# Starting the norm of image 1 when the scans end, in a two-layer SSM and attention kernel

## The chip, the cores and the metric

The kernel runs on one core of a Trainium2 chip, in one launch. A core has TensorE (PE, matrix products), VectorE (DVE), ScalarE (ACT), GpSimd (POOL) and the sync engine (SP), each with an instruction queue of its own that runs in order, and 16 DMA engines that move data between HBM and the on-chip memory. A DMA stands in the queue of the engine that issues it: its waits are spent there. The metric is the device time of one execution in microseconds (us), as the median of several runs. The profile is one execution seen by the hardware profiler.

## The reference

The input x is 4 images of 96 channels and 128 x 128 points, in float32. Two layers are added to it, each behind a group norm `_gn` (32 groups of 3 channels).

Layer 0 is a state-space block:

```python
z = silu(dwconv3x3(in_w @ gn(x) + in_b) + dw_b)       # 192 channels
xs = [z, z transposed, and both reversed]             # 4 directions, L = 16384
dts, B, C = x_proj(xs)                                # rank 6, 1, 1
delta = softplus(dt_proj(dts) + bias);  dA = exp(delta * A)
h[t] = dA[t] * h[t-1] + delta[t] * B[t] * xs[t]       # the scan
y = h * C + D * xs                                    # summed over directions
x = x + out_w @ layernorm_over_channels(y) + out_b
```

Layer 1 is a convolutional attention block on the new x:

```python
xr, x1, x2 = relu_split_norm(gn(x))       # two passes: statistics, then two maps
key, qry = unfold(conv3x3(x1, aw1)), unfold(conv3x3(x2, aw2))
w = softmax(sum over patches(key * qry) / sqrt(96 * 9))    # a 96 x 96 x 3 x 3 filter per image
y1 = layernorm(conv3x3(conv3x3(x1, aw3), w))
y2 = layernorm(conv3x3(x2, w_conv2)) * x1
x = x + xr + w_full @ [y1, y2] + b_full
```

All of it is computed for each image. No image needs another's result; within an image each norm needs the whole image before it.

## The kernel before, in words

The work is written as Python generators, each of which emits instructions and yields an estimate of the TensorE time that they cost. `co_run(left, right, pace)` draws from a left generator, and for each unit of its cost lets the right one emit `pace` units. Two are thus woven into one stream.

**Projections** (`project`, L612): image after image, in 16 strips of 8 rows. A strip is loaded (`strip_in`), normalised in place on ScalarE (`stacked`, L455), copied with shifts by DMA (L463), and multiplied on TensorE in three groups `q` of seven terms `i`. The group norm of an image needs its statistics first: `image_stats` loads the image in 32 tiles (`xst`, L401) and takes `bn_stats` on VectorE (L404). Image 0's are taken ahead; those of images 1 to 3 run `beside` the projection of image 0, a half tile at each `next(beside, None)`.

**Scans** (`ssm_scan`): 384 steps of 1024 points on 128 channels. A step has products that spread B, C and delta (`to_psum`, L726), softplus and exp on ScalarE (L655, L788), a multiplication by u on GpSimd (`times_u`, L812), two halves of multiply, scan, multiply on VectorE (L816, L833, L837), and an addition into y on GpSimd (`into_y`, L845). The scans are the right generator `last` beside the projections, then beside the norm of image 0 (pace 0.5), then beside the nine taps of image 0 (pace 0.95).

**Norm** (`Image.norm`): `ssm_output`, then `split_norm`. `ssm_output` goes over 16 chunks of 1024 points. For chunk c it loads y (`load_y`, L929), squares it on ScalarE (`squares`, L934), sums y and its squares over the channels on TensorE (`sums`, L940), copies the sums out (`rows`, L950) and turns them into an 8 x 128 tile `mq` with two small DMAs (L953). One chunk later it takes the variance (`inverse`, L957 to L959), the root (`roots`, L963) and the reciprocal (`back`, L967), writes that to memory (`rd`, L969) and reads it back spread over 96 partitions (`spread_out`, `r`, L977). One chunk later still it projects (`projected`, L983), scales and adds (`scaled`, L991 to L993) and stores x (L1028). `split_norm` then makes two passes: relu and sums (L1077 to L1084), a small chain of single-column operations with one product (L1093), and the maps x1 and x2 (L1160, L1165), which are written to memory.

**Nine taps** (`direct_maps`, L1646): the three 3 x 3 convolutions of image 0 as nine shifted products each, strip by strip of three rows, with `Taps` turning the results (L1383) and multiplying patches (L1398). Its end is the softmax of the weights (`Taps.weights`, L1446 to L1462).

**Attention**: `attention(img)` does the same convolutions for images 1 to 3 in another form (L1288, L1299), with input sums made on GpSimd and VectorE (`columns`, L1264 to L1273), and for every image the convolution with the softmax weights. Beside the attention of image b run, as right generator `light`, the closing stage of image b-1 (`attn_output`) and the norm of image b+1.

What sets the order: from the first projection to the end of the scans and nine taps, `in_order` ties every instruction to the one emitted before it on its engine, so the written order is the order. Behind that point a scheduler chooses an order on each engine by its own estimates. The norm of image 0 draws its product banks from a pool of three (`psl`), the norms of images 1 to 3 from a pool of two (`psr`). All DMAs of these stages stand in the sync queue, apart from the weight tables (L246, L249), which GpSimd issues.

Of the kernel before, what the change touches and what calls it, by code (L numbers as in the profile page):

```python
# [14 lines left out]
PSUM = bass.MemoryType.PSUM  # L15
# [47 lines left out]
def kernel(  # L63
# [271 lines left out]
    def chain(*gens):  # L335
        for g in gens:
            yield from g

    def drain(gen):
        for _ in gen:  # L340
            pass
# [48 lines left out]
    def image_stats(b, pool):  # L390

        stats = pool.tile([C, NCH, 6], F32, name="stats", tag="stats")
        mv = const.tile([C, 2], F32, name=f"stats{b}", tag=f"stats{b}")

        def run(p2, ahead):
            xf = x[b].rearrange("c h w -> c (h w)")
            tiles = []
            for i in range(NCH + ahead - 1):
                if i < NCH:
                    tiles.append(p2.tile([C, CH], F32, name="xst", bufs=ahead))  # L400
                    nc.sync.dma_start(tiles[-1], xf[:, bass.ts(i, CH)])  # L401
                yield 0.7
                if i >= ahead - 1:
                    nc.vector.bn_stats(stats[:, i - ahead + 1], tiles.pop(0))  # L404
                yield 0.7
            nc.vector.bn_aggr(mv, stats.rearrange("p c s -> p (c s)"))

        return mv, run

    def project(b, weights, mv, beside, zb, xrows, ps):  # L410
# [8 lines left out]
        SP = ZR * PW + 2  # L419
        last = H // ZR - 1  # L420
        with tc.tile_pool(name="a2", bufs=2, side="left") as p2:
            beside = chain(*(run(p2, 2) for run in beside))
            later, parts = Later(), {}
            y0s = []
            for i in range(2):
# [173 lines left out]
            for s in range(last + 1):  # L599
                nxt = None  # L600
                z1 = p2.tile([128, NU, ZR, UW], F32, name="z1")
                z2 = p2.tile([128, NU, R, UW], F32, name="z2")
                for q in range(3):
                    pz = bank(ps)
                    for i, (k, d) in enumerate(terms):
                        n = C + KK + 1 if k == 2 else 128
                        if q < 2:
                            jobs = [(0, 128, 0, q)]
                        else:
                            jobs = [(0, 64, 128, 0), (64, 128, 128, 1)]  # L610
                        for p, e, c, at in jobs:
                            nc.tensor.matmul(  # L612
                                blocks(pz[p:e]),
                                lhsT=ws[k][:, d, c : c + e - p],
                                rhs=window(ys[k], at, d, n),
                                start=(i == 0),
                                stop=(i == len(terms) - 1),
                            )
                        if i in (2, 4, 6):
                            yield tick(2.6 if i == 2 else 1.8)  # L620
                        if i == 2 and q == 0 and s < last:
                            ahead = strip_in(s + 1)
                        if i in (2, 4, 6):
                            next(beside, None)
                    to = z1[:, :, q * R : (q + 1) * R] if q < 2 else z2
                    silu(to.rearrange("p b h w -> p b (h w)"), pz)
                    if q == 0 and s < last:
                        nxt = stacked(s + 1, *ahead)
                    if q == 1:
                        if before:  # L630
                            rp = rows_out(*before)
                            later(lambda a=before: z_out(*a), 1)
                            yield tick(1.8)
                        for _ in range(3):
                            next(beside, None)
                    if q == 2 and before:
                        cols_out(rp, before[2])
                        yield tick(1.3)
                before = z1, z2, s
                ys = nxt  # L640
                ready[b] = s - 1
# [272 lines left out]
    def ssm_output(b, yms, xnew, stats, ps, side):  # L914
# [5 lines left out]
        with tc.tile_pool(name="c2", bufs=2, side=side) as p2:  # L920
# [10 lines left out]
            def squares(c):  # L931
                sq = p2.tile([C, 2, SN], F32, name="sq", bufs=1)
                for j in range(2):
                    nc.scalar.activation(sq[:, j], ys[c][:, j], AF.Square)  # L934
                sums_of[c] = sq, bank(ps)
# [12 lines left out]
            def rows(c):  # L948
                st = p2.tile([128, CH], F32, name="st", bufs=1)
                nc.scalar.copy(st, sums_of.pop(c)[1])  # L950
                mq = made[c] = p2.tile([RS, 2, W], F32, name="mq")
                for i in range(2):
                    nc.sync.dma_start(mq[:, i], st[32 * i : 32 * i + 65 : 64])  # L953

            def inverse(c):
                m, q = made[c][:, 0], made[c][:, 1]
# [8 lines left out]
            def back(c):  # L965
                q = made.pop(c)[:, 1]
                nc.vector.reciprocal(q, q)  # L967
                to = rd[bass.ts(c, SN)]
                nc.sync.dma_start(to.rearrange("(p f) -> p f", f=W), q)  # L969
                xr = p2.tile([C, SN], F32, name="xr")  # L970
                nc.sync.dma_start(xr, xb[:, bass.ts(c, SN)])
                near[c] = xr, to

            def spread_out(c):
                xr, to = near[c]
                r = p2.tile([C, SN], F32, name="r")
                nc.sync.dma_start(r, to.partition_broadcast(C))  # L977
                near[c] = xr, r

            def projected(c, h):  # L980
# [17 lines left out]
            for c in range(NS + 2):  # L998
                new, old = c < NS, c - 2 if c >= 2 else None
                mid = c - 1 if 1 <= c <= NS else None  # L1000
                if old is not None:
                    po = projected(old, 0)
                yield 1.2
                if mid is not None:
                    inverse(mid)
                    roots(mid)
                if new:
                    squares(c)
                if old is not None:
                    scaled(old, 0, po)  # L1010
                    po = projected(old, 1)
                    ys.pop(old)
                if mid is not None:
                    back(mid)
                yield 1.4
                if new:
                    sums(c, 0)
                if mid is not None:
                    spread_out(mid)
                yield 1.4  # L1020
                if old is not None:
                    scaled(old, 1, po)
                    load_y(c + 1)
                if new:
                    sums(c, 1)
                yield 1.4
                if old is not None:
                    nc.sync.dma_start(xnew[:, bass.ts(old, SN)], near.pop(old)[0])  # L1028
                yield 1.4
                if new:  # L1030
                    rows(c)
                yield 1.4
# [766 lines left out]
    def projections(images, weights, stats, wp, ps):  # L1799
        for b in images:  # L1800
            beside = []
            for i in range(1, NB) if b == 0 else ():
                stats[i], run = image_stats(i, wp)
                beside.append(run)
            yield from project(
                b, weights, stats[b], beside, zb[b // 2][b % 2], xrows[b], ps
            )
            ready[b] = H // ZR
# [4 lines left out]
    with tc.tile_pool(name="wp", bufs=1, side="left") as wp:  # L1813
# [1 line left out]
        stats[0], run = image_stats(0, wp)  # L1815
        weights = project_weights(wp)
        with tc.tile_pool(name="a0", bufs=8, side="right") as p2:
            drain(run(p2, 8))
        first = len(traced())
        others = other_weights()  # L1820
        for images, pace in (([0], 0.25), ([1], 0.75), ([2, 3], 1.35)):
# [18 lines left out]
    co_run(left, last, 0.5)  # L1840
    drain(left)
    left = direct_maps(imgs[0], psl)
    co_run(left, last, 0.95)
    drain(left)
    drain(last)
    in_order(first)
    early.close()
    istats.append(ctx.enter_context(tc.tile_pool(name="istats1", bufs=1, side="left")))
    const = ctx.enter_context(tc.tile_pool(name="const2", bufs=1, side="left"))
    wful = load(w_full, "wful")  # L1850
    m96 = filled(1.0 / C, "m96", 128, 128)
# [4 lines left out]
        nc.vector.memset(mrows[i][0:64], rows / (H * C))  # L1856
        nc.vector.memset(mrows[i][64:128], (H - rows) / (H * C))
    psl = ctx.enter_context(tc.tile_pool(name="psa", bufs=6, space=PSUM, side="left"))
    psr = ctx.enter_context(tc.tile_pool(name="psr", bufs=2, space=PSUM, side="right"))
    wp = ctx.enter_context(tc.tile_pool(name="wpairs", bufs=1, side="left"))  # L1860
    pairs = [stacked_weights(wp, wd, f"wd{i}") for i, wd in enumerate(four)]
    for b in range(NB):
        light = []
        if b:
            light.append(imgs[b - 1].close(psr, "right"))
        if b + 1 < NB:
            imgs[b + 1] = Image(b + 1)
            light.append(imgs[b + 1].norm(yms[(b + 1) // 2][(b + 1) % 2], psr, "right"))
        light = chain(*light)
        left = imgs[b].attend(psl)  # L1870
        co_run(left, light, 0.5 if b else 1.5)
        drain(left)
        drain(light)
# [76 lines left out]
```

## Time and profile before

The median of 3 runs is 6911.25 us (6910.0 to 6920.79). The profiled execution spans 6917.3 us.

| stage, us from the start | length | TensorE busy | clock granted |
|---|---|---|---|
| projections, 0 to 2090 | 2090 | 1771 | 0.93 |
| norm of image 0 beside scans, 2090 to 2571 | 481 | 240 | 0.60 |
| nine taps beside scans, 2571 to 3361 | 790 | 750 | 0.98 |
| rest of the nine taps, 3361 to 3436 | 75 | 75 | 1.00 |
| softmax of image 0's weights, 3436 to 3487 | 51 | 27 | 0.64 |
| output of image 0 beside norm of image 1, 3487 to 3908 | 421 | 270 | 0.76 |
| attention of image 1, 3908 to 4946 | 1038 | 868 | 0.91 |
| attention of image 2, 4946 to 5989 | 1043 | 873 | 0.90 |
| attention of image 3 and closing, 5989 to 6917 | 928 | 788 | 0.93 |

Over the whole span TensorE is busy 82%, VectorE 71%, ScalarE 42%, GpSimd 49%. The stages have different limits, so the table is to be read row by row. A wait in the profile is named by the waiting instruction, then what ended the wait, then the total, the count and the longest in us. `issue` is time in which the engine waited for nothing that the profile shows.

### The profile page before, as it was taken

Reading aid. Unit: us, or ns where it says so; the run is one execution under the profiler, and the core shown is the slowest. Engines: PE = TensorE matmul, PEld = TensorE weight load, DVE = VectorE, ACT = ScalarE, POOL = GpSimd, SP = SyncE. Lnnn points to the kernel's source line nnn. Section 1 sums busy time; section 2 is a strip of 40 time slices with the busy share of each in tenths; the row PEclk is TensorE's granted clock in tenths of the full one; section 3 lists DMA queues with packets and bytes.
Section 4 is the critical chain, followed back from the end, with each engine's and each line's share of the span. In section 5 each row is a group of like instructions: output and inputs, shape, how many; then the busy total and the mean of one; then the engine's idle time right before and its main releaser. Section 6 shows DMA issues by size and latency. Waiting matters only on the chain. (4 is left out here: it accounts for less than half of the span.)

```text
span 6917.3 us, 74304 instructions
## 1 busy us (share of the span) xinstructions
PE 5662.7 (82%) x22236; PEld 2330.5 (34%) x22236; DVE 4920.7 (71%) x6916; ACT 2913.8 (42%) x3685; POOL 3397.6 (49%) x2072
## 2 busy tenths in 40 slices
PE   5879979878886629999977488987788987888987
PEld 2323323322221114444422234443334442334432
DVE  3357779989896678788466675568765568775688
ACT  1247778777875476676312321232121232121102
POOL 1126758879794239778222233434433334444641
PEclk9989989989996659999978799997899997899998
DMA  7666677866766666766567765667665666565556
GB/s 171 169 155 172 177 208 199 232 170 171 218 181 169 182 200 193 200 180 175 163 183 192 201 167 149 181 169 202 172 166 146 178 170 201 157 173 137 139 155 175
DMA packets 798510, 1227.60 MB, mean 177 GB/s; under 512 B 217726, under 2 KB 557702, under 8 KB 785628
## 3 DMA queue, kind: packets, MB, share of 16 engines
q1 hardware_dynamic: 795212, 1222.45, 64.8%
q8 instruction: 179, 2.93, 0.2%
q14 instruction: 223, 1.83, 0.1%
q0 software_dynamic: 2896, 0.39, 0.1%
HBM read 858.12 MB, written 296.46 MB: 167 GB/s over the span
## 5 line engine op out<-in xcount | busy, mean ns | idle before, releaser
L1264 POOL TENSOR_TENSOR t<-y 128x768 f32<-128x768 f32 (+1 forms) x352 | 557.4, 1584 | 1915.2 <-DMA y<-vd 530.0
L612 PE MATMUL bank<-y,wp 128*128 128x512 f32 (+3 forms) x3584 | 1331.6, 632 | 69.1 <-DVE z L488 26.3
L845 POOL TENSOR_TENSOR y<-y,dl 128x1024 f32<-128x1024 f32 x384 | 1054.6, 2746 | 485.4 <-DVE dl L837 442.7
L812 POOL TENSOR_TENSOR dl<-dl,u 128x1024 f32<-128x1024 f32 x384 | 1006.9, 2622 | 493.7 <-ACT dA L788 242.1
L1288 PE MATMUL bank<-t,wd 128*128 128x384 f32 (+2 forms) x4224 | 1120.2, 491 | 34.4 <-ACT s L1337 15.0
L833 DVE TENSOR_TENSOR_SCAN dA<-dA,pBC 128x512 f32<-128x512 f32 x768 | 981.7, 1278 | 30.6
L1337 ACT COPY s<-bank 128x384 f32<-128x384 f32 (+2 forms) x292 | 136.0, 466 | 1985.7 <-PE bank L1299 1942.0
L1288 PE MATMUL bank<-t,wa 128*96 128x384 f32 (+1 forms) x1408 | 574.4, 557 | 199.8 <-DVE t L1265 130.1
L1288 PEld LDWEIGHTS bank<-t,wd 128*128 128x128 f32 (+1 forms) x4224 | 551.5, 168 | 549.9 <-issue 292.1
L837 DVE TENSOR_TENSOR dl<-dA,pBC 128x512 f32<-128x512 f32 x768 | 528.6, 688 | 290.0 <-PE pBC L726 223.1
L612 PEld LDWEIGHTS bank<-y,wp 128*128 128x128 f32 (+3 forms) x3584 | 463.8, 171 | 749.1 <-issue 661.9
L1646 PE MATMUL bank<-y,wn 128*128 128x384 f32 (+5 forms) x2408 | 652.8, 497 | 37.7 <-DMA y<-x1d 19.1
L726 PE MATMUL pBC<-xr,wbc 60*128 60x512 bf16 (+1 forms) x1536 | 439.4, 402 | 279.3 <-DVE dA L833 222.3
L1329 DVE TENSOR_TENSOR d<-s,bank 128x384 f32<-128x384 f32 (+2 forms) x292 | 156.2, 535 | 657.0 <-ACT s L1337 582.7
L655 ACT ACTIVATE dl<-pd,dtb 128x512 f32<-128x512 f32 x768 | 486.3, 684 | 166.8 <-PE pd L726 149.9
L816 DVE TENSOR_TENSOR pBC<-dl,pBC 128x512 f32<-128x512 f32 x768 | 527.3, 687 | 3.1 <-POOL dl L812 1.9
L788 ACT ACTIVATE dA<-dl,negA 128x1024 f32<-128x1024 f32 x384 | 420.3, 1141 | 2.3
L1288 PEld LDWEIGHTS bank<-t,wa 128*96 128x96 f32 x1408 | 245.6, 188 | 513.4 <-issue 293.9
L1646 PEld LDWEIGHTS bank<-y,wn 128*128 128x128 f32 (+3 forms) x2408 | 303.5, 165 | 306.7 <-issue 137.2
L1265 POOL TENSOR_TENSOR t<-y 128x384 f32<-128x384 f32 (+1 forms) x352 | 396.3, 1126 | 0.0
L1266 POOL TENSOR_TENSOR t<-y 128x384 f32<-128x384 f32 (+1 forms) x352 | 364.1, 1034 | 0.0
L655 ACT ACT_TABLE_LOAD x245 | 314.3, 1283 | 94.8 <-PE pd L726 91.3
(254 smaller groups left out, 7529.0 us busy)
## 6 DMA issues: line engine op xcount, KB each, us to landing
u<-zb SPq DMA_DIRECT2D x192, 1024.0 KB
yms<-y SPq DMA_DIRECT2D x96, 512.0 KB
y<-yms SPq DMA_DIRECT2D x64, 768.0 KB
xn<-xnew SPq DMA_DIRECT2D x128, 384.0 KB
y<-y SPq DMA_DIRECT2D x128, 258.2 KB
zb<-z SPq DMA_DIRECT2D x64, 512.0 KB
y<-vd SPq DMA_DIRECT2D x168, 193.8 KB
y<-in_x SPq DMA_DIRECT2D x56, 480.0 KB
```

Source lines behind the costliest of these rows:

```text
L612: nc.tensor.matmul(blocks(pz[p:e]), lhsT=ws[k][:, d, c : c + e - p], rhs=window(ys[k], at, d, n), start=(i == 0), stop=(i == len(terms) - 1),)
L655: nc.scalar.activation(dst, src, AF.Softplus, bias=bias)
L726: nc.tensor.matmul(p, lhsT=w[rows], rhs=xr[rows, at : at + CH], start=True, stop=True)
L788: nc.scalar.activation(live[m]["dA"], live[m]["dl"], AF.Exp, scale=negA[:, g % 3, k : k + 1])
L812: nc.gpsimd.tensor_mul(t, t, u_view(n))
L816: nc.vector.tensor_mul(p, live[n]["dl"][:, bass.ts(half, CH)], p)
L833: nc.vector.tensor_tensor_scan(h, h, p, init, ALU.mult, ALU.add)
L837: nc.vector.tensor_mul(live[n]["dl"][:, sl], live[n]["dA"][:, sl], live[n]["C", half])
L845: nc.gpsimd.tensor_add(v, v, t.rearrange("p (a b) -> p a b", b=W))
L1264: eng.tensor_sub(v[:, 0:2], of(y, 0), of(y, 2))
L1288: nc.tensor.matmul(pc[p:e, :n], lhsT=w[:, i, c : c + e - p], rhs=t[k][:, i, :n], start=(k == 0), stop=False,)
L1646: nc.tensor.matmul(pc[p:e, :n].rearrange("p (h w) -> p h w", w=W), lhsT=w[:, c : c + e - p], rhs=v[:, :, 0:W], start=(i == 0), stop=(i == ...
```

## The change

Four things are changed together.

1. **The norm of image 1.** The scans run beside the nine taps at pace 1.15 in place of 0.95, so that they are all emitted while a part of the nine taps is left. The written order ends there. The norm of image 1 is created at this point and woven with the rest of the nine taps at pace 1.0; what is left of it runs beside the attention output of image 0. The scheduler orders all of this.
2. **Queues in the norm.** The two DMAs into `mq` are issued by ScalarE, those of `rd` and `r` by GpSimd. In each chunk the squares are emitted ahead of the inverse and the roots.
3. **Statistics.** Those of images 1 and 2 run beside the projection of image 0 with their loads issued by GpSimd, those of image 3 beside the projection of image 1 with loads issued by sync.
4. **Strips.** The normalisation of the next strip (`stacked`) is emitted in the middle of group q = 1 in place of the end of q = 0.

The aim is to give TensorE other work while the norm of image 1 runs, and to take waits out of the sync queue.

```diff
         with tc.tile_pool(name="a2", bufs=2, side="left") as p2:
-            beside = chain(*(run(p2, 2) for run in beside))
+            each = len(beside)
+            beside = chain(*(run(p2, 2, queue) for run, queue in beside))
...
-                        if i in (2, 4, 6):
+                        if i == 2 and q == 1 and s < last:
+                            nxt = stacked(s + 1, *ahead)
+                        if i in (2, 4, 6)[:each]:
                             next(beside, None)
...
-                    if q == 0 and s < last:
-                        nxt = stacked(s + 1, *ahead)
...
-                        for _ in range(3):
+                        for _ in range(each):
                             next(beside, None)
...
-                    nc.sync.dma_start(mq[:, i], st[32 * i : 32 * i + 65 : 64])
+                    nc.scalar.dma_start(mq[:, i], st[32 * i : 32 * i + 65 : 64])
...
-                nc.sync.dma_start(to.rearrange("(p f) -> p f", f=W), q)
+                nc.gpsimd.dma_start(to.rearrange("(p f) -> p f", f=W), q)
...
-                nc.sync.dma_start(r, to.partition_broadcast(C))
+                nc.gpsimd.dma_start(r, to.partition_broadcast(C))
...
                 yield 1.2
+                if new:
+                    squares(c)
                 if mid is not None:
                     inverse(mid)
                     roots(mid)
-                if new:
-                    squares(c)
...
-            for i in range(1, NB) if b == 0 else ():
+            for i in {0: range(1, NB - 1), 1: (NB - 1,)}.get(b, ()):
                 stats[i], run = image_stats(i, wp)
-                beside.append(run)
+                beside.append((run, nc.sync if b else nc.gpsimd))
...
     left = direct_maps(imgs[0], psl)
-    co_run(left, last, 0.95)
-    drain(left)
+    co_run(left, last, 1.15)
     drain(last)
     in_order(first)
+    istats.append(ctx.enter_context(tc.tile_pool(name="istats1", bufs=1, side="right")))
+    psr = ctx.enter_context(tc.tile_pool(name="psr", bufs=2, space=PSUM, side="right"))
+    imgs[1] = Image(1)
+    next_norm = imgs[1].norm(yms[0][1], psr, "right")
+    co_run(left, next_norm, 1.0)
+    drain(left)
     early.close()
-    istats.append(ctx.enter_context(tc.tile_pool(name="istats1", bufs=1, side="left")))
...
-    psr = ctx.enter_context(tc.tile_pool(name="psr", bufs=2, space=PSUM, side="right"))
...
-        if b + 1 < NB:
+        if b + 1 == 1:
+            light.append(next_norm)
+        elif b + 1 < NB:
             imgs[b + 1] = Image(b + 1)
```

More of the change, by code (lines that the diff above doesn't have):

```diff
@@ L393, in image_stats, with run @@
         mv = const.tile([C, 2], F32, name=f"stats{b}", tag=f"stats{b}")
-        def run(p2, ahead):
+        def run(p2, ahead, queue):
             xf = x[b].rearrange("c h w -> c (h w)")
@@ L400, in run @@
                     tiles.append(p2.tile([C, CH], F32, name="xst", bufs=ahead))
-                    nc.sync.dma_start(tiles[-1], xf[:, bass.ts(i, CH)])
+                    queue.dma_start(tiles[-1], xf[:, bass.ts(i, CH)])
                 yield 0.7
@@ L1817 @@
         with tc.tile_pool(name="a0", bufs=8, side="right") as p2:
-            drain(run(p2, 8))
+            drain(run(p2, 8, nc.sync))
         first = len(traced())
```

## The prediction

> **What bounds the kernel now.** I read the slices of the page first, then cut the span at the stage boundaries that the first and last start of each line give: projections until 2090 us (L612), norm of image 0 until 2571, nine taps beside the scans until the last scan at 3361 (L833), the rest of the taps until 3436 (L1646), the softmax of the weights until 3487, attention output of image 0 beside the norm of image 1 until 3908 (first L1288 product of image 1). Busy time by stage; columns are length, PE, PEld, DVE, ACT, POOL (busy us and count), clock, DMA share, GB/s:
>
> ```profile
> 2090.00:2571.00 481.00, 239.87 (x606) 56.17 (x602) 339.63 (x465) 273.87 (x323) 150.48 (x97) 0.60 0.64 185
> 2571.00:3361.00 790.00, 749.71 (x3273) 363.25 (x3273) 647.42 (x792) 513.03 (x659) 619.65 (x231) 0.98 0.66 189
> 3361.00:3436.00 75.00, 75.00 (x359) 42.31 (x358) 9.72 (x19) 18.17 (x34) 2.35 (x1) 1.00 0.52 132
> 3436.00:3487.00 51.00, 27.05 (x75) 8.45 (x73) 29.98 (x58) 11.93 (x15) 9.74 (x8) 0.64 0.69 186
> 3487.00:3908.00 421.00, 270.37 (x847) 99.69 (x847) 290.20 (x502) 118.62 (x169) 85.36 (x101) 0.76 0.70 193
> 3908.00:4946.00 1038.00, 867.94 (x3694) 395.43 (x3695) 714.26 (x1115) 239.00 (x350) 405.08 (x363) 0.91 0.65 174
> ```
>
> TensorE bounds the taps stage (95%) and its tail (100%). Two stages leave it idle: the norm of image 0 (50%, clock 0.60) and the 421 us in which image 1's norm outlasts image 0's output (64%, clock 0.76). The waits inside the norm of image 0 (2150 to 2390) say why the first is slow:
>
> ```profile
> ACT mq L963 <- DVE mq L959: 106.2, 15, 10.5
> DVE mq L957 <- DMA mq<-st: 68.9, 14, 9.0
> ...
> PEld bank L940 <- ACT sq L934: 52.0, 24, 5.4
> ```
>
> One chunk on ScalarE, by the timeline, shows the order behind them:
>
> ```profile
> 2283.09 0.40 ACT L963 ACTIVATE mq<-mq,eps 8x128 f32<-8x128 f32 x1 [5.80 <-DVE mq L959]
> 2283.40 1.99 ACT L934 ACTIVATE sq<-y 96x1024 f32<-96x1024 f32 x2
> 2285.40 1.28 ACT L655 ACT_TABLE_LOAD   x1
> 2286.70 1.27 ACT L655 ACTIVATE dl<-pd,dtb 128x512 f32<-128x512 f32 x2
> 2288.22 0.59 ACT L950 COPY st<-bank 128x512 f32<-128x512 f32 x1 [0.26 <-ACT dl L655]
> ```
>
> A ring: the statistics of a chunk are copied (L950), turned by two small DMAs (L953), reduced on VectorE (L957), rooted (L963); only then, in the same queue, come the squares of the next chunk (L934), its sums on TensorE (L940) and its copy. The 16 copies go from 2137 to 2370, so 15.5 us a chunk. For the second idle stage, the waits of TensorE (3487 to 3908):
>
> ```profile
> PE bank L1699 <- DMA y<-x1d: 41.7, 1, 41.7
> PE bank L183 <- DVE mv L180: 33.2, 1, 33.2
> PE bank L1288 <- DVE t L1265: 29.7, 9, 10.7
> PE bank L1288 <- DMA wa<-watd: 18.8, 1, 18.8
> PE bank L940 <- DVE r L991: 18.0, 5, 7.2
> ```
>
> The first two are the end: attention is done at 3857, image 1's maps land at about 3900. The waits of the sync queue add what holds all loads behind it:
>
> ```profile
> SPq L969 <- DVE mq L967: 456.2, 62, 18.3
> ```
>
> **What the Trainium skill says.** "DMA: Bandwidth & Descriptors", section Anatomy of one DMA, says that a wait before a DMA is spent in the issuing sequencer, not in the DMA engines: so L969's 456 us stand in the sync queue, and the change puts them into GpSimd's. The trace agrees that the queue stands. The same page's Specifications give about 1 us to the first byte for a DMA that GpSimd issues and 0.6 us from sync or ScalarE; the trace has GpSimd issues only in the weight loads (54 of L246 in 30.2 us, 0.56 us each, 4.1 us to landing). "SBUF — State Buffer" says of the port pair that VectorE and GpSimd share that one blocks until the other's instruction ends; the trace fits: an L957 of 0.28 us took 2.26 us at 2280.23, ending with GpSimd's multiply. "TensorE: Matmul & The Clock Gate", Part 1, says that idle TensorE falls to half clock; the 0.60 in the norm agrees.
>
> **The change part by part.**
>
> *Projections.* The statistics of images 1 and 2 are loaded by GpSimd beside image 0, image 3's by sync beside image 1. 64 issues of 0.56 us are 36 us of GpSimd, which was busy 34 us of the 248 from 188 to 436: hidden. In the built program the 66 weight copies (L246, L249) stand ahead of the next statistics load, and VectorE, in order, waits for that load ahead of the z that frees TensorE's bank: before it waited until 174, now until about 188 (147 plus 66 issues of 0.56 plus 4 to land), so up to 14 us worse. Against that the sync queue loses half its statistics, and ScalarE's wait at L455 for the strip (143 us in all, mostly hidden) goes, because the strip is normalised some ticks later. I take 0; ends -15 and +15. Image 3's 32 L404 of 0.68 us add 22 us to VectorE beside image 1, 75% busy: hidden by TensorE's 97%.
>
> *Norm of image 0.* Squares now precede the inverse and the root, so L940 needs no root; the two L953 go out on ScalarE right after their own copy. Gone from the ring: 2.0 us of squares and the sums behind them, and 1 to 4 us that L953 stood behind other sync work. Added: two issues of about 0.5 us on ScalarE (57% busy), rd and r on GpSimd (31% busy). What remains: VectorE's own work, some 10 us a chunk, still meets the wait for mq, since TensorE's scan products keep it in step with VectorE. 0 to 4 us less a chunk; I take 2.2, times 16: -35 us (0 to -60). The added wait: r's load stands in GpSimd until rd has landed, 3 to 4 us, with the scan's multiply (L812) queued behind and VectorE's L816 behind that. At one scan step a chunk there are some 10 us of slack.
>
> *Taps beside scans, pace 0.95 to 1.15.* In the built programs TensorE has 1074 tap products ahead of the last scan product and 130 after it; the change makes it 882 and 322. So 192 leave this stage. At 140 products in 77 us (3150 to 3250) one is 0.55 us: 106 us. The stage has 116.5 scan steps (233 L833), 6.78 us each, TensorE 6.43; without 0.91 it is 5.5. The next bound is read where projections and scans run with the same loads: from 1100 to 1460 57.5 steps took 6.26 us each, with TensorE 5.6, VectorE 5.7, GpSimd 5.3. In the taps stage GpSimd is slower (5.3 a step on average, 6.0 from 2650 to 2750), so I take 6.4: -44 us (6.2 gives -68, 6.6 gives -21).
>
> *After the scans.* Before: 547 us from 3361 to 3908. Now: 322 products at 0.5 us (148 records, 74 products, in 35.7 us from 3361 to 3400) are 161; turning the taps, 9 us per 130, 22; image 1's sums and projections 131 (L940 and L983 took 122 us for 12.5 chunks at clock 0.84). Sum 314, at 92% busy 341. The first pass (L1077, 57 us from 3763) ends later than the 40 us of taps that stand ahead of its L1093 on TensorE: with the start 20 more. So 361. Softmax of the weights 51 as before. Output of image 0: image 3 shows it alone, 147 us (6644 to 6791) with VectorE at 139.7; the second pass has 41 us of L1165, half beside the softmax: 160. To the next product 15 (4931 to 4946). Sum 587: +40 us. At 97% busy and no wait it is 548 (0), at 85% and a 20 us longer tail 633 (+86). The 41.7 us wait at the end is gone in all of these; it is eaten by 192 products that now stand here. No GpSimd work stands behind rd and r there.
>
> *Norms of images 2 and 3* lie beside attention with TensorE 92% busy. The sync queue is freer; GpSimd, where L1264 to L1266 stand behind rd and r, was idle over half. I take -8 for both; ends -40 and +50.
>
> Sum: 6911 - 35 - 44 + 40 - 8 = 6864.
>
> **The rivals.** (1) *Everything overlaps*: norm chunks at 11.7 us, scans at 6.2, no cost after: 6911 - 60 - 68 - 15 = 6768 to 6800. For it: from 3430 to 3462, with the scans over, four copies of image 1 stand 10.6 us apart. Against: VectorE's 10 us a chunk, and the second pass with 230 to 250 GB/s. (2) *Only moved*: the 192 products come back in full and the ring keeps its mq wait: -44 + 40 to 50 and -10 from the norm, 6897 to 6925. For it: 68.9 us of mq wait are not removed by either edit. (3) *GpSimd becomes the in-order trap, slower*: 2 us more in each of 16 chunks of image 0 (32), r later by 2 us in 32 chunks of images 2 and 3, where two banks hold L983 (up to 50), less 44 and plus 40 as above: 6911 + 78 = 6989, half of it 6950. For it: sync's 7 us mean wait at L969, now ahead of GpSimd's columns; GpSimd also waits 229 us for x1d and x2d between 4210 and 4610, and r would stand behind. Against: L1288 waited only 3 us for GpSimd there.
>
> **How the numbers follow.** Forecast (6805 to 6897) 0.57; rival 1 0.14; rival 2 0.16; rival 3 0.13. The range, 6790 to 6930, takes in most of rival 2 and the edge of 1. Over 0.2% is 14 us: faster below 6897, slower above 6925. Faster 0.57 + 0.14 + a little of rival 2 = 0.75; same 0.11; slower 0.14.
>
> **What would show it.** Copies of image 0's norm nearer 13 us than 15.5, with fewer L940 waits on L934; last scan near 3280 at 6.4 us a step; first attention product of image 1 near 3870 with no wait of 40 us on x1d; a wait at L1093 of 15 to 20 us. I am wrong if GpSimd's wait for rd shows ahead of L812 or L1264 with VectorE or TensorE behind it, or if TensorE after the scans stays under 85% busy.

## The result, and the profile after

The changed kernel takes 6869.06 us (median of 4 runs, 6861.66 to 6886.88) against 6910.62 us for the kernel before: a ratio of 0.9944, with a 95% interval of 0.9919 to 0.9969. The forecast was 6864 us. The total came out 5 us from it; several of its terms lie further off. From here on lines are those of the changed kernel, one higher than before in the functions concerned; the profiled execution spans 6859.9 us.

The stages of the changed kernel, cut at the same events as before. Columns: stretch and length, then busy us and instructions of PE, PEld, DVE, ACT, POOL, then TensorE clock, DMA share, GB/s.

```profile
0.00:2079.00 2079.00, 1764.38 (x6293) 591.65 (x6293) 1524.16 (x1946) 1351.52 (x1577) 1364.28 (x649) 0.93 0.69 186
2079.00:2545.00 466.00, 217.13 (x600) 53.08 (x599) 359.66 (x462) 273.32 (x321) 164.65 (x128) 0.60 0.67 191
2545.00:3270.00 725.00, 671.09 (x2823) 311.96 (x2825) 636.61 (x774) 497.13 (x627) 616.51 (x231) 0.97 0.67 193
3270.00:3567.00 297.00, 273.41 (x1164) 124.49 (x1160) 136.22 (x280) 111.57 (x190) 18.98 (x37) 0.97 0.69 186
3567.00:3618.00 51.00, 4.41 (x23) 2.67 (x21) 35.34 (x51) 18.05 (x19) 10.70 (x17) 0.56 0.85 241
3618.00:3830.00 212.00, 169.52 (x545) 70.82 (x546) 187.91 (x270) 32.90 (x43) 91.96 (x90) 0.88 0.72 205
3830.00:4884.00 1054.00, 884.20 (x3693) 399.12 (x3693) 765.68 (x1111) 238.94 (x349) 411.51 (x394) 0.90 0.64 171
4884.00:5944.00 1060.00, 885.28 (x3689) 399.58 (x3688) 769.06 (x1106) 236.58 (x347) 415.56 (x398) 0.89 0.63 169
```

Set against the terms of the prediction (lengths in us, from the profiles):

| term | before | after | measured | predicted |
|---|---|---|---|---|
| projections | 2091 | 2079 | -12 | 0 |
| norm of image 0 | 480 | 466 | -14 | -35 |
| taps beside scans | 790 | 725 | -65 | -44 |
| after the scans, to image 1's first attention product | 547 | 560 | +13 | +40 |
| images 1, 2, 3 | 1039, 1044, 926 | 1054, 1060, 916 | +15, +16, -10 | -8 in all |

The sum is -57, the difference of the two spans; the medians are 42 us apart. The execution profiled before is 8 us above its median and the one after 7 us below, so some 15 us in these rows may be spread between executions and not the change. The gain is where the prediction put it: TensorE gave up 192 tap products beside the scans and took them back behind them, where the norm of image 1 had left it idle. The row to look at twice is image 1's and 2's. TensorE does the same there, but VectorE's busy time rose from 714 and 712 us to 766 and 769 with almost the same number of instructions, so its instructions became longer.

Two waits show what the queues did in the norm of image 0 (2150 to 2390; who waited, for what, us in total, times, longest):

```profile
POOL rd L970 <- DVE mq L968: 87.4, 14, 8.2
...
ACT sq L935 <- DMA y<-yms: 48.3, 10, 9.4
POOL r L978 <- DMA rd<-mq: 42.2, 10, 7.5
...
DVE mq L958 <- DMA mq<-st: 9.2, 5, 3.1
```

VectorE's wait for the small DMAs into `mq`, 68.9 us before, is 9.2. GpSimd now stands 130 us for `rd` and `r`. ScalarE's squares wait for y, a wait that was not among the first before: the ring has shifted to the next slowest part.

Behind the scans, TensorE's waits up to the end of the taps (3270 to 3567), then in the output of image 0 (3567 to 3830):

```profile
PE bank L1647 <- ACT ring L1661: 11.5, 2, 5.7
PE bank L1094 <- DVE c L1092: 5.2, 1, 5.2
```

```profile
PE bank L1289 <- DMA wa<-watd: 34.8, 1, 34.8
PE bank L1289 <- DVE t L1266: 27.0, 7, 9.8
```

The 41.7 us wait for x1d at the end is gone. The wait at L1094 is 5.2 us, not 15 to 20. In its place the softmax weights come back from memory later (34.8 us where it was 18.8): their load was issued at 3614, beside the reads and writes of image 1's second pass, with the DMA engines 85% busy from 3567 to 3618.

### The profile page after: what moved, and what is told of

The parts are those of the page before. It is cut to its first block, busy times and chain, and to the rows that moved or that the text cites. A ratio compares the mean times of both kernels' runs of the same rounds, so it can differ in the third digit from the quotient of the medians.

```text
span 6859.9 us, 74337 instructions
## 1 busy us (share of the span) xinstructions
PE 5650.5 (82%) x22236; PEld 2322.2 (34%) x22236; DVE 5060.8 (74%) x6916; ACT 2912.9 (42%) x3685; POOL 3478.8 (51%) x2264
## 5 line engine op out<-in xcount | busy, mean ns | idle before, releaser
L613 PE MATMUL bank<-y,wp 128*128 128x512 f32 (+3 forms) x3584 | 1317.0, 626 | 94.2 <-DVE z L489 38.6
L1289 PE MATMUL bank<-t,wd 128*128 128x384 f32 (+2 forms) x4224 | 1145.5, 496 | 78.3 <-DVE s L1331 20.6
L846 POOL TENSOR_TENSOR y<-y,dl 128x1024 f32<-128x1024 f32 x384 | 1051.4, 2738 | 258.6 <-DVE dl L838 228.3
L1289 PEld LDWEIGHTS bank<-t,wd 128*128 128x128 f32 (+1 forms) x4224 | 557.2, 170 | 622.0 <-issue 323.4
L727 PE MATMUL pBC<-xr,wbc 60*128 60x512 bf16 (+1 forms) x1536 | 459.9, 403 | 349.6 <-DVE dA L834 276.2
L838 DVE TENSOR_TENSOR dl<-dA,pBC 128x512 f32<-128x512 f32 x768 | 528.1, 688 | 272.3 <-PE pBC L727 199.8
L1289 PE MATMUL bank<-t,wa 128*96 128x384 f32 (+1 forms) x1408 | 561.3, 548 | 202.8 <-DVE t L1266 128.7
L1647 PE MATMUL bank<-y,wn 128*128 128x384 f32 (+5 forms) x2408 | 670.2, 505 | 38.4 <-ACT ring L1661 16.1
L1289 PEld LDWEIGHTS bank<-t,wa 128*96 128x96 f32 x1408 | 241.0, 184 | 507.9 <-issue 305.6
L1266 POOL TENSOR_TENSOR t<-y 128x384 f32<-128x384 f32 (+1 forms) x352 | 382.2, 1086 | 0.0
L727 PEld LDWEIGHTS <-wbc 60*128 60x128 bf16 (+1 forms) x1536 | 103.5, 96 | 781.7 <-issue 767.6
```

What stands on the lines that cost most here:

```text
L613: nc.tensor.matmul(blocks(pz[p:e]), lhsT=ws[k][:, d, c : c + e - p], rhs=window(ys[k], at, d, n), start=(i == 0), stop=(i == len(terms) - 1),)
L727: nc.tensor.matmul(p, lhsT=w[rows], rhs=xr[rows, at : at + CH], start=True, stop=True)
L838: nc.vector.tensor_mul(live[n]["dl"][:, sl], live[n]["dA"][:, sl], live[n]["C", half])
L846: nc.gpsimd.tensor_add(v, v, t.rearrange("p (a b) -> p a b", b=W))
L1289: nc.tensor.matmul(pc[p:e, :n], lhsT=w[:, i, c : c + e - p], rhs=t[k][:, i, :n], start=(k == 0), stop=False,)
L1647: nc.tensor.matmul(pc[p:e, :n].rearrange("p (h w) -> p h w", w=W), lhsT=w[:, c : c + e - p], rhs=v[:, :, 0:W], start=(i == 0), stop=(i == ...
```

## Experiments

Each time is a median; each ratio is to the kernel before on the same chip, with its 95% interval.

**The parts by themselves.** Part 1 alone, on the kernel before (the other three as before):

> Part 1 alone on the kernel before: pace 1.15, written order ends with the scans, norm of image 1 woven with the rest of the nine taps; queues, statistics and strips as before. Theory: the scans' stage shrinks by 55 to 65 us (6.2 us a step), what follows them grows by 12 to 35 us because the sync queue still holds the mq copies back, image 2's and 3's norms as before: 6911 - 60 + 25 = 6876, and the stages of images 1 and 2 stay at 1038 and 1043 us. Rival (the start of the norm needs the freed sync queue): chunks of image 1 stay at 18 to 20 us, the stretch after the scans grows by 60 or more, and the time is 6905 to 6920.

Measured: 6894.89 us, 0.9975 (0.9964 to 0.9987): 18 us gained, half of what the theory had. The scans' stage went from 790 to 726 us, as it said, and after the scans it was 577 (+30), near the predicted +40. But image 1's stage did not stay: it was 1055, with no DMA of the norm on GpSimd at all, so its lengthening alone convicts nobody. Image 2's was 1041.

Part 2 alone:

```diff
-                nc.sync.dma_start(mq[:, i], st...)
+                nc.scalar.dma_start(mq[:, i], st...)
-                nc.sync.dma_start(to..., q);   nc.sync.dma_start(r, ...)
+                nc.gpsimd.dma_start(to..., q); nc.gpsimd.dma_start(r, ...)
+                if new: squares(c)      # ahead of inverse and roots
```

> Part 2 alone on the kernel before: mq by ScalarE, rd and r by GpSimd, squares ahead of the roots. Theory: 20 to 30 us less in the norm of image 0, about 15 us more in each of the stages of images 1 and 2, because VectorE's operations with two inputs from SBUF stand for 5 to 12 us behind GpSimd's load of r and the work after it; the sum is 6905 to 6920. Rival (the loss beside images 1 and 2 comes from the shifted start of the norm or of the scheduler's order, not from the queues): both stages stay at 1038 and 1043, and the time is 6880 to 6890.

Measured: 6905.91 us, 0.9996 (0.9984 to 1.0007): no gain as a whole, as the theory of this run had it, but not by its sum. The norm of image 0 took 465 in place of 480, and behind the projections VectorE had 20 instructions of over 4 us, where the kernel before has none there; 16 of them lie beside attention. Yet the stages of images 1 and 2, for which the theory had 15 us more each, took 1047 and 1038 in place of 1039 and 1044. (The profiled execution is 16 us faster than the median.)

Parts 3 and 4 alone:

> Parts 3 and 4 alone on the kernel before: statistics split over images 0 and 1 with GpSimd loading beside image 0, and the later normalisation of the strips. Theory: the projections end 12 us earlier and nothing else changes: 6899. Strip 4 of image 0 takes 60 us in place of 42 (statistics behind 66 weight copies in GpSimd's queue), strips 9 to 15 take 29 us less. Rival (the 12 us are of the scans' start or of noise): the projections end within 4 us of 2091 and the time is 6907 to 6915.

Measured: 6908.38 us, 0.9992 (0.9982 to 1.0002). The strips of image 0 are as the theory had them: the fifth takes 61 us, the last seven 191 in place of 220. Of its 12 us at the end of the projections 2 to 8 show: they ended at 2083, where the profiles of kernels with unchanged projections have 2085 to 2091. The time lies in the rival's range. The three ratios multiply to 0.9963, inside the interval of the whole. So no interplay of the parts shows, though one of under some 20 us could hide in these intervals; nearly all that shows is part 1's.

**What moved the norm of image 0.** The squares alone, with all queues as before:

> The kernel before with the squares emitted ahead of the inverse and the roots, and no queue changed. Theory: the 2.0 us of squares behind the root are what leaves the ring of the norm of image 0: a chunk takes 13.5 to 14.5 us in place of 15.6, the stage 465 to 472 in place of 480, time 6893 to 6905. Rival: the ring is held by the two small DMAs in the sync queue, which stay: 15.2 to 15.6 us a chunk, time 6906 to 6914.

Measured: 6914.92 us, 1.0007 (0.9999 to 1.0016), 15.9 us a chunk. The rival has it. The waits of this run (2150 to 2390) show why:

```profile
ACT sq L934 <- DMA y<-yms: 103.8, 13, 13.9
DVE mq L957 <- DMA mq<-st: 61.2, 14, 8.7
...
ACT mq L963 <- DVE mq L959: 18.2, 8, 8.0
```

ScalarE's wait at the root fell from 106 to 18 us and came back as 104 us for y, whose loads stand in the sync queue behind `rd` (129.6 us of waiting there). So the order on ScalarE alone was not the limit; the next runs show that the queues matter. Whether the early squares help once the queues are freed was not run.

**The DMAs of `rd` and `r`.** The changed kernel with both back on sync:

> The changed kernel with L969 and L977 (rd and r) back on the sync queue for all images; mq stays on ScalarE, squares stay early. Theory (GpSimd's load of r locks VectorE out): no VectorE operation of this stage over 4 us, VectorE's busy time beside images 1 and 2 back from 766 and 769 to about 714, those stages 14 to 18 us shorter each, the norm of image 0 some 10 us shorter: 6869 - 40 = 6829. Rival (sync's wait for the reciprocal costs what the lock did): those stages fall by under 5 us, loads of x1d and x2d come later, 6860 to 6880.

Measured: 6839.03 us, 0.990 (0.988 to 0.992): 30 us *better* than the whole change. No VectorE instruction is over 4 us any more; images 1 and 2 take 1040 and 1031. Against the theory two things got worse: a chunk of image 0's norm is 14.9 us (13.9 with GpSimd), and after the scans it takes 578 (560).

Then with GpSimd for images 0 and 1 and sync for images 2 and 3, `(nc.gpsimd if b < 2 else nc.sync)`:

> The changed kernel with the writes of rd and the loads of r issued by GpSimd for images 0 and 1 only, by sync for images 2 and 3. Theory: the place decides. In the norms of images 0 and 1 GpSimd's queue helps (470 back to 466, 578 after the scans back to 559), beside attention, where GpSimd goes on with input sums, it costs (stages of images 1 to 3 at 1040, 1031, 926 as with both on sync). That is 6839 - 4 - 19 = 6816, and VectorE has instructions of over 4 us only in the norm of image 0 (about 7). Rival: the 578 was the scheduler's other order and not the sync queue; then this run is as with both on sync, 6835 to 6843.

Measured: 6835.35 us, 0.9883 (0.9861 to 0.9904). By stage 465, 568, 1042, 1033: each where the theory had it but for 568, half of the hoped step. The total can't be told from the version before it.

Only `r` back on sync, `rd` by GpSimd:

> The changed kernel with only the loads of r back on sync; rd is still written by GpSimd, which waits for VectorE's reciprocal as before. Theory: the load of r (96 rows of 4 KB) is what makes VectorE stand: no VectorE instruction of over 4 us is left, the stages of images 1 and 2 are near 1040 and 1035, time 6835 to 6855. Rival: any wait or DMA in GpSimd's queue does it: 15 to 21 instructions over 4 us stay and the time is 6860 to 6875.

Measured: 6891.24 us, 0.9975 (0.9965 to 0.9985). Both failed. Most of the long instructions went, 6 of 21 stayed, the longest 12.5 us; so it does not take a large transfer, as `rd` is only 8 rows of 512 bytes. And the time is worse than with both on either queue. Behind the scans sync's `r` waits for the `rd` that GpSimd writes: 35.3 us in seven waits between 3276 and 3858, a stretch that takes 584 us where it took 560. The stages of images 1 and 2 stay as long as in the changed kernel, 1061 and 1054, though VectorE's busy time in them is back at 716 and 715 us.

The other way round, on the kernel before, a load of the size of `r` by GpSimd that waits for nothing but its buffer:

```diff
-                nc.sync.dma_start(xr, xb[:, bass.ts(c, SN)])
+                nc.gpsimd.dma_start(xr, xb[:, bass.ts(c, SN)])
```

> The kernel before with one thing changed: the load of xr (96 rows of 4 KB, read from the input, nothing to wait for but its buffer) is issued by GpSimd in all four norms. Theory: a load of this size issued by GpSimd makes VectorE's instructions with two inputs stand while GpSimd works on behind it, whether anything waits for rd or not: 15 to 40 VectorE instructions of over 4 us, stages of images 1 and 2 longer by 5 to 20 us each, time 6910 to 6940. Rival: it takes the spreading of one row to 96 partitions, or the wait for rd, to do it: none over 4 us, time 6895 to 6912.

Measured: 6919.44 us, 1.0009 (0.9996 to 1.0022). Nine instructions behind the projections are over 4 us, eight of them in the norm of image 0 and one beside attention. So no broadcast and no wait for `rd` is needed, but without such a wait it happens seldom beside attention. The last section comes back to it.

**The statistics' loads** beside image 0 on sync again, all else as changed:

```diff
-                beside.append((run, nc.sync if b else nc.gpsimd))
+                beside.append((run, nc.sync))
```

> The changed kernel with the statistics' loads beside image 0 issued by sync again. Theory: strip 4 of image 0 (60 us, of which 18 were VectorE behind GpSimd's 66 weight copies) comes back to about 42 us, and most of it reaches the end of the projections: 2079 becomes 2065 to 2070, time 6855 to 6862. Rival: the sync queue then holds the strips and image 0's later strips lose the 29 us that they had gained: projections end at 2085 to 2095, time 6872 to 6885.

Measured: 6837.03 us, 0.9884 (0.9862 to 0.9907), 32 us better than the whole change; the projections end at 2057. The direction is the theory's, the size twice what it had. The fifth strip of image 0 takes 41.9 us before, 60.1 in the changed kernel, and 31.6 here. VectorE's wait for the first loaded tile between 140 and 200, in the changed kernel and then in this run:

```profile
DVE stats L404 <- DMA xst<-in_x: 40.9, 1, 40.9
```

```profile
DVE stats L404 <- DMA xst<-in_x: 28.3, 6, 13.1
```

The rival (late strips lose what they had gained) falls short: the last seven strips take 199 us, where they took 191 in the changed kernel and 220 before. So most of their gain, 21 of 29 us, is not the queue's; it comes from the fewer statistics beside image 0 or from the later normalisation of the strips, which weren't taken apart.

**Together**, statistics on sync and `rd`, `r` on sync for images 2 and 3:

> Two repairs of the changed kernel together: the statistics' loads beside image 0 issued by sync, and rd and r by sync for images 2 and 3. Theory: the two losses are in different stages and add up, 6869 - 32 - 34 = 6803 (6797 to 6812), projections ending near 2060, stages of images 1 and 2 near 1042 and 1033. Rival: the slack that one repair frees is the same that the other uses, or the profiled stages differ by chance from run to run: 6820 to 6837.

Measured: 6822.87 us, 0.9872 (0.9858 to 0.9885). The repairs do not add up: 46 us of 66, so the rival has it. The stages are as the theory had them (2061, 1040, 1038), but with the statistics on sync the stages of images 1 and 2 had already been 1050 and 1044 with GpSimd's loads still in them, not 1054 and 1060: less was left to win.

The same with ScalarE in place of sync for `rd` and `r`, `(nc.gpsimd if b < 2 else nc.scalar)`:

> The same two repairs, but with rd and r of images 2 and 3 issued by ScalarE in place of sync. Theory: what hurt was GpSimd working on right behind its DMAs; another queue without a share in that port does no harm and also keeps the sync queue free: equal to the version with sync or up to 10 us better, no VectorE instruction over 4 us beside attention. Rival: a queue that waits for rd holds up its own engine whatever it is; ScalarE's copies that TensorE waits for come late and it is 10 to 30 us slower than the version with sync.

Measured: 6773.82 us, 0.9801 (0.9787 to 0.9814), the best of all, 95 us faster than the changed kernel. The theory had at most 10 us over sync; it is 49. As it said, no VectorE instruction beside attention is over 4 us, but with sync there is none either, so that can't be the difference. Images 1 and 2 in the version with sync, then in this one:

```profile
3822.00:4862.00 1040.00, 871.97 (x3694) 399.45 (x3693) 709.39 (x1111) 239.59 (x349) 396.95 (x363) 0.90 0.64 173
4862.00:5900.00 1038.00, 873.99 (x3688) 400.39 (x3687) 704.45 (x1106) 237.26 (x347) 405.32 (x365) 0.89 0.64 172
```

```profile
3814.00:4838.00 1024.00, 873.55 (x3695) 394.83 (x3694) 710.21 (x1111) 238.48 (x349) 396.99 (x362) 0.91 0.65 176
4838.00:5855.00 1017.00, 868.89 (x3689) 395.21 (x3688) 706.43 (x1107) 236.12 (x347) 409.77 (x368) 0.91 0.65 176
```

Each engine's busy time is the same within 6 us; what went is idle time. In the profile of every run here, the stages of images 1 and 2 end 44 to 47 us after the start of ScalarE's last map (L1161) of the *next* image's norm. The first product of the next image reads these maps, so the stage lasts as long as that norm. Its steps in the stage of image 1, from the stage's start:

| kernel | `rd`, `r` of images 2, 3 | first copy | last copy | last statistics | last map | end |
|---|---|---|---|---|---|---|
| before | sync | 311 | 665 | 699 | 995 | 1039 |
| changed | GpSimd | 317 | 672 | 711 | 1009 | 1054 |
| both repairs | sync | 312 | 655 | 700 | 994 | 1040 |
| both repairs | ScalarE | 317 | 641 | 680 | 978 | 1024 |

With ScalarE the 16 copies span 324 us in place of 343 with sync, 1.3 us less a chunk, and the norm ends 16 us earlier. In the changed kernel they span 355, as before, though its squares and `mq` are the quicker ones: GpSimd's part eats that, and takes 5 us more from the last copy to the last statistics.

The traces show where `rd` stood. With sync it went out 17 us after the reciprocal on average (16 chunks, norm of image 2), with GpSimd (the changed kernel) 1.0 us, with ScalarE at once. One chunk with sync, then one with ScalarE (start, duration, operation):

```profile
4387.37 0.94 DVE L968 RECIPROCAL mq<-mq 8x128 f32<-8x128 f32 x1 [0.47 <-ACT mq L964]
4396.26 13.52 SPq L1481 DMA_DIRECT2D c2d<-ring  x2
4409.88 0.28 SPq L970 DMA_DIRECT2D rd<-mq  x1
```

```profile
4260.70 0.94 DVE L968 RECIPROCAL mq<-mq 8x128 f32<-8x128 f32 x1 [0.47 <-ACT mq L964]
4261.68 0.28 ACTq L970 DMA_DIRECT2D rd<-mq  x1
```

In the sync queue `rd` comes behind attention's own loads and stores (here L1481, in these two runs' numbering). From a chunk's copy to its first scaling it takes 40 us with sync, 34 in the changed kernel and 30 with ScalarE. How ten us less in each chain become 1.3 us less between chunks is not shown; the chain alone does not set it, as GpSimd has a shorter one than sync and a longer norm.

**More of the same pace**: 1.35 for 1.15 in the version with sync.

> The two repairs (with sync) and the scans beside the nine taps at pace 1.35 in place of 1.15: 443 in place of 322 tap products stand behind the last scan product in the built program. Theory: the gain of the pace is used up, since a step is then bound by VectorE and GpSimd: 121 x 0.55 = 66 us of TensorE leave the scans' stage, which shortens by 15 to 35 us, and come back nearly in full behind it: 20 to 45 us slower than at 1.15. Rival: behind the scans the products still fall into holes of TensorE beside the norm of image 1: -35 + 20, 15 us faster.

Measured: 6812.94 us, 0.9862 (0.9846 to 0.9877), not to be told from 6822.87. The scans' stage fell by 33 us and the stretch behind it grew by 51, as the theory had it, but its total (20 to 45 us slower) failed: the stages of images 1 and 2 came out 15 and 8 us shorter in this profile. Why they did is open.

## Why the prediction came out as it did

- **Taps beside scans, -44: right mechanism, undersized.** A step took 725 / 116.5 = 6.22 us, the lower end (6.2) of the step's range. TensorE was still at 93% there. GpSimd, whose 5.3 busy us a step made me take 6.4, was busy 85% of the stage (616 us) and did not hold the step there.
- **After the scans, +40: right sign, oversized by 27.** Of the sum 361 + 51 + 160 + 15 the first term failed: it was 297. Its parts were sized well (the norm's products 131 us in the trace, the taps 172 for 161, turning 19 for 22), but they sum to 322 where TensorE's busy time in the stretch is 273: a product's recorded duration overlaps its neighbour's, so a sum of durations is no length. The first pass (L1078) also ran beside taps, from 3515 to 3558, and the wait behind it was 5 us, not 20. The last two terms, 175, came to 212, with the 34.8 us for the weights in it.
- **Norm of image 0, -35: oversized.** A chunk went from 15.6 to 13.9 us, 1.7 where the step took 2.2; over the 15 intervals 25 us. The step's reason "gone from the ring: 2.0 us of squares" failed: alone they bring nothing. What helped were the queues, the other reason given: with early squares and `mq` on ScalarE, and `rd` and `r` still on sync, a chunk takes 14.9 us; with these on GpSimd too 13.9. Of the 25 us, some 10 went back at the end: from the last copy to the last statistics (L994) it takes 34 us in place of 23, and 21 with `rd` and `r` on sync.
- **Projections, 0 with ends of 15: both halves right, the balance off.** The wait for the tile that is loaded behind the 66 weight copies lasted to 192.8, near the 188 of the step, and cost 18 us in that strip; the later strips gained 29. The experiment prices the choice of queue at about 20 us of projections.
- **Norms of images 2 and 3, -8: wrong sign.** The step "lie beside attention with TensorE 92% busy" failed, twice. By the row shown there it is 868 of 1038 us, 84%; and it took the busiest engine for the bound. The stage ends 44 to 47 us after the next norm's last map in every run, so what slows that norm slows the stage. The two stages with these norms beside them took 31 us more where the step had 8 less.
- **Rival 3**, GpSimd as an in-order trap, named two places, and one was right. In image 0's norm GpSimd's waits (130 us in the waits above) did not slow the chunks: over the whole stage its wait for L838 ahead of L846 fell from 166.7 to 42.2 us in exchange. Beside attention it lost, with 31 us for its up to 50. Part of its mechanism is there: `r` goes out 6.3 us after the reciprocal where it was 1.9. But TensorE waited only 0.4 us for GpSimd's columns (L1289 for L1266, stage of image 1), so the loss did not come by late columns. A sign that the prediction named against itself, a wait for `rd` ahead of L1264 with VectorE behind it, did show.
- **Rival 2**: its terms add up to 6897 to 6907, not to 6925, and its ground, that no edit removes the 68.9 us of `mq` wait, was wrong: 9.2 us were left.

So the near hit in the total was luck, of errors that cancel: by the profiles 21 + 27 + 12 us better than thought, 21 + 29 worse. That leaves 10 us better; the medians, 15 us closer together than the profiled executions, make it 5 worse.

What GpSimd cost beside attention is known less well than the ratios suggest. The same norm code gave lengths of images 1 and 2 that differ by some 30 us between profiles (with `rd` and `r` by GpSimd 2114 in the changed kernel, 2094 with only the statistics moved, 2085 with part 2 alone; with both on sync 2071 to 2078; the kernel before has 2083). Nor is VectorE's standing, which the last section describes, shown to be what lengthened them: with part 2 alone VectorE was busy 765 and 757 us and the stages were as in the kernel before; with only `r` on sync it was busy 716 and 715 and they were as long as in the changed kernel. Which wait behind GpSimd's queue costs the norm its time is open. Image 3's stage is 915 to 917 us in some kernels and 923 to 930 in others, with no tie to a queue; that is open.

## What to carry to other kernels

- Before costing an edit in a stage, find the event that its end follows by a constant distance in every run. Here it was the last map of the next image's norm, with TensorE 84% busy beside it.
- A DMA that waits for a result stands behind all that its queue holds, and all that comes later stands behind it. Choose the queue by both. With all else equal, `rd` and `r` of images 2 and 3 gave 6837 us on GpSimd, 6823 on sync and 6774 on ScalarE, which was 23% busy there; the DMA stood 17 us in sync's queue and not at all in ScalarE's.
- Put first loads of a stage in a queue that has nothing long ahead of them: 66 weight copies cost 18 us of the strip that needed one tile.

## What the hardware did that was not expected

In these traces, after a DMA issued by GpSimd, an instruction of VectorE can stand for as long as GpSimd goes on without a gap. GpSimd in the changed kernel, from the DMA on, and VectorE over the same time (start, duration, operation):

```profile
4272.51 0.54 POOL L978 DMA_DIRECT2D r<-rd  x1 [2.15 <-DMA y<-x2d]
4273.06 1.48 POOL L1265 TENSOR_TENSOR t<-y 128x768 f32<-128x768 f32 x1
4274.50 0.83 POOL L1266 TENSOR_TENSOR t<-y 128x384 f32<-128x384 f32 x1
...
4280.50 0.82 POOL L1266 TENSOR_TENSOR t<-y 128x384 f32<-128x384 f32 x1
4281.28 0.81 POOL L1267 TENSOR_TENSOR t<-y 128x384 f32<-128x384 f32 x1
```

```profile
4272.87 9.65 DVE L1274 SCALAR_TENSOR_TENSOR t<-y,signs 64x384 f32<-64x384 f32 x1
4282.55 0.55 DVE L1330 TENSOR_TENSOR d<-s,bank 128x384 f32<-128x384 f32 x1
```

Nine instructions of GpSimd pass, and L1274 ends 0.4 us after the last. In the kernel before, a row of twelve such instructions lets VectorE in between: GpSimd, then VectorE's lines of the same kind.

```profile
4277.77 0.82 POOL L1265 TENSOR_TENSOR t<-y 128x384 f32<-128x384 f32 x1
4278.56 1.14 POOL L1266 TENSOR_TENSOR t<-y 128x384 f32<-128x384 f32 x1
4279.66 1.47 POOL L1264 TENSOR_TENSOR t<-y 128x768 f32<-128x768 f32 x1
```

```profile
4278.33 0.68 DVE L1271 TENSOR_TENSOR t<-y 64x384 f32<-64x384 f32 x1
...
4279.97 1.57 DVE L1273 SCALAR_TENSOR_TENSOR t<-y,signs 64x384 f32<-64x384 f32 x1
```

Counted over images 1 and 2: of VectorE's instructions L1272, L1274 and L993 (each with an operand pair in on-chip memory), 19 began in a gapless row directly behind a GpSimd DMA and had over 2.6 us of it ahead; 17 of them stood until 0.4 to 0.6 us after the row's end, 143 us in all, up to 12.7. In rows that no DMA precedes 38 began, and none took over 1.91 us. In the kernel before, it is none of 74. With part 2 alone 16 of 22 stood behind a DMA, and none of 39 in the other rows. So it takes the DMA and a row of work directly behind it; a wait in GpSimd's queue lets such work pile up, which would explain why `xr`, with no wait, did it once beside attention and `rd`, with one, five times. In the norm of image 1 (3287 to 3486), where GpSimd has nothing to do, there is none.

"SBUF — State Buffer", section "SBUF: two separate sides", says in the Trainium skill that VectorE and GpSimd lock a port pair for one whole instruction. The kernel before agrees: there no such instruction took over 1.96 us. Behind a GpSimd DMA the measurement goes further: the pair was not handed over for up to twelve instructions. Why the DMA makes that difference no run here shows.
